# A sparse attention layer on one core: list extraction with three segments a quarter row, and later statistics, pinned scans and scatters

## The chip, the cores and the metric

The kernel runs on 1 core of one Trainium2 chip. The metric is device microseconds of one execution. Three runs of the kernel before gave 1813.75, 1815.98 and 1820.42 us; the median is 1815.98 us. One further execution was taken by the hardware profiler, and everything below that speaks of a place in time counts from the start of its span.

## The reference

One transformer layer over a graph of 4096 nodes, D = 512, 8 heads of 64, all in float32. Keys and values come from `x`, queries from `h_target`; the edge mask is the integer matrix `adj` (4096 x 4096, about 17 ones in a row).

```python
hs = layer_norm(x);  ht = layer_norm(h_target)
q = ht @ Wq / 8;  k = hs @ Wk;  v = hs @ Wv          # (4096, 8, 64)
logits = where(adj != 0, q . k, -1e30)
ctx = softmax(logits) @ v
ht = layer_norm(ht + ctx @ Wo)
y = ht + gelu(ht @ W1) @ W2                          # 512 -> 2048 -> 512
out = normalise(x + y)
```

## The kernel before, in words

Only the edges that exist are computed. The first stage makes two things from HBM: `kvd`, a table with k and v of every source row (4 KB a row), and for every target row a list of its edges. The second stage takes target rows in tiles of 128, sorted by degree, fetches one k|v row per target and list place with an indirect DMA ("a gather", 128 rows of 4 KB, 512 KB), and does attention and the feed-forward part.

**k|v** (`project`, `source`, L861 to L961). A source tile of 128 rows is normalised, transposed, and multiplied with Wk and Wv on PE (L930); ACT copies the two products out of PSUM (L932), and a DMA that ACT issues stores them to `kvd` (L936). There are 32 such tiles. PSUM has three buffers for the products (`pq`).

**Lists** (`edges`, L717 to L762). A target tile's row of `adj` comes in four quarters of 1024 columns, 512 KB each, loaded by SP (L714). For each quarter ACT writes sign bytes and their row sum (L729), DVE views two bytes as one 16 bit word and multiplies it with the word's place in its segment (`lio`, L734), and a MAX8 takes the eight largest words of each segment (L736). With `SQ = 5` a quarter's 512 words make 5 segments of at most 103 words; the place of a word goes up in steps of two, so that one byte holds it. After four quarters, a tile's 4 x 5 x 8 words are parted into bytes (L743, L744), turned into column numbers `gid`, 320 wide (L748, L751), and three MAX8 with two MATCH_REPLACE8 between them give the 24 largest (L755, L757). What is left over is written to HBM (`rest_d`, L767), for the few rows with a longer list.

The 32 target tiles are two parts of 16 (A, B). After part A's lists comes `sort(0)` (L809 to L858): a counting sort by degree on DVE, with four small products on PE, then 16 scatters by POOL that write each row's record (degree, row number, the two layer norm factors, the list) to its sorted place (L854). Records are then loaded, sorted, by POOL (L980). Part B goes the same way in `sort(1)`, but its lists are made beside the attention of part A.

**Statistics of h_target** (`moments`, L796 to L803): DVE's mean and variance of each target row, for the layer norm factors of the record. Two tiles are done per list (L738), so that all 32 are ready with part A's 16 lists. The rows lie in four slots of a ring of 20 buffers of 512 KB; the same ring later holds the gathered rows.

**Attention** (`attention`, L1160 to L1253). Per three gathers (a "segment"): a DVE product with q (L1220), a DVE reduction to logits `lg` (L1225), ACT's exponential (L1229, or L1238 for a tile's first segment), weighting of v on DVE (L1184) and, for one row in three, on ACT (L1201, L1204), and sums on PE by transposing products into `cps` (L1192). A tile's last segment starts `finish` (output projection, second norm), which ends with `h2T` of a group of one or two tiles. The feed-forward part (`feed`: L1325, gelu L1328, L1334) runs on those groups, woven between the attention's instructions.

**What sets the order.** Streams of work are Python generators, each of which yields an estimated cost; `_weave` takes the stream that is least far on. The first weave (L1438) has `projections`, `prepare` (part A's lists, sort, records, the first two queries) and `fill` (the next `FILL = 5` lists of part B). The second (L1449) has attention, feed-forward, `other_lists` (the remaining 11 lists and `sort(1)`; it begins at `WAIT = 40`, its costs are multiplied by 1.5) and the last weights. The framework's scheduler may then move an instruction ahead on its engine, unless `tc.issue_after` ties it behind another one. Each engine runs its instructions in the order that comes out, and so does each issuing queue. The number of quarters that may be loaded ahead is set by `RINGED`: tiles below it use the 8 ring slots 0 to 7, later ones two other buffers (`wide`).

## Time and profile before

| what | us |
|---|---|
| median of three runs | 1815.98 |
| the profiled execution, its own time | 1817.49 |
| its span | 1815.5 |
| PE busy in the span | 1677.8 (92%) |
| DVE busy | 1436.5 (79%) |
| ACT busy | 1224.1 (67%) |
| POOL busy | 982.2 (54%) |
| last k\|v product on PE ends | 280.6 |
| last k\|v store issued by ACT | 290.6 |
| first gather issued by POOL | 296.6 |
| first feed-forward product on PE | 373.5 |
| part B's scatters | 627 to 665 |
| last gathers land, attention ends | about 1670 |

The page gives each engine's busy time, a row of 40 slices in which a digit is a slice's busy share in tenths, the groups of instructions with the mean time of one, and the idle time before a group with what ended most of it. A table by windows gives busy time per engine for stretches that one chooses. A timeline gives single instructions: start, duration, engine, line, operation, tiles, and in brackets how long the engine had been idle and who released it. PE's busy time has to be read with care, since ends of matmuls are modelled and they overlap; idle time of PE is safe to read.

### The profile page before, as it was taken

What the parts mean: (1) busy time and instruction counts of PE and PEld (TensorE: products, weight loads), DVE (VectorE), ACT (ScalarE), POOL (GpSimd) and SP (SyncE); (2) the same over time, 40 slices, a digit from 0 to 9 for tenths busy, and PEclk for the clock granted to TensorE, in tenths of its full rate; (3) what the DMA queues carried; (4) which work ended last, traced back from release to release, by engine and by line L of the source; (5) the groups of instructions that cost most, each with busy time, mean ns of one, the idle gap of its engine ahead of it and who ended that gap; (6) DMA issues with size and microseconds to landing.
All of it is one profiled execution on the core that took longest, in us unless ns stands there. A gap on an engine that the chain in (4) does not pass through costs nothing. (4 is left out here: it accounts for less than half of the span.)

```text
span 1815.5 us, 22973 instructions
## 1 busy us (share of the span) xinstructions
PE 1677.8 (92%) x7030; PEld 1097.9 (60%) x7030; DVE 1436.5 (79%) x2660; ACT 1224.1 (67%) x3121; POOL 982.2 (54%) x834
## 2 busy tenths in 40 slices
PE   7989984597999979999999989999999999999997
PEld 3434442465766656766776757666666666666664
DVE  6989876899999837777978989978878797988200
ACT  5767654487987736766778868877777676787311
POOL 1000144656566676766678788867575665763101
PEclk9999996698999989999999999999999999999998
DMA  9999968989887557777878878787776776774000
GB/s 344 366 380 372 344 198 319 404 287 332 271 305 256 201 173 243 258 255 267 273 263 302 293 260 295 249 285 250 241 266 222 248 251 238 244 248 153 18 6 26
DMA packets 140269, 463.26 MB, mean 255 GB/s; under 512 B 16500, under 2 KB 21672, under 8 KB 140136
## 3 DMA queue, kind: packets, MB, share of 16 engines
q0 software_dynamic: 96656, 342.64, 55.8%
q1 hardware_dynamic: 35664, 95.98, 15.0%
q10 hardware_dynamic: 7816, 23.08, 3.3%
q8 instruction: 58, 0.95, 0.2%
q14 instruction: 75, 0.61, 0.1%
HBM read 430.75 MB, written 30.89 MB: 254 GB/s over the span
## 5 line engine op out<-in xcount | busy, mean ns | idle before, releaser
L967 POOL DMA_INDIRECT kv<-kvd,rec x603 | 758.1, 1257 | 347.5 <-PE cps L1192 139.7
L1334 PE MATMUL po<-w,gt 128*128 128x512 f32 x1024 | 466.4, 598 | 16.2 <-ACT gt L1328 16.2
L1325 PE MATMUL pf<-h2T,w 128*128 128x256 f32 (+1 forms) x2176 | 465.9, 368 | 0.1
L1325 PEld LDWEIGHTS pf<-h2T,w 128*128 128x128 f32 x2176 | 389.3, 191 | 64.5 <-issue 20.3
L1220 DVE TENSOR_TENSOR kv<-kv,tq 128x1536 f32<-128x1536 f32 (+2 forms) x211 | 351.6, 1675 | 68.3 <-DMA kv<-kvd,rec 56.2
L1204 ACT ACTIVATE kv<-kv,pa 128x64 f32<-128x64 f32 x1520 | 391.0, 336 | 4.3
L1225 DVE TENSOR_REDUCE lg<-kv 128x24 f32<-128x1536 f32 (+2 forms) x211 | 350.1, 1666 | 1.4
L1334 PEld LDWEIGHTS po<-w,gt 128*128 128x128 f32 x1024 | 188.8, 192 | 212.4 <-issue 194.3
L1192 PEld LDWEIGHTS cps<-ident,kv 128*128 128x128 f32 x2008 | 240.2, 145 | 109.4 <-issue 59.2
L1192 PE MATMUL cps<-ident,kv 128*128 128x128 f32 x2008 | 264.5, 280 | 44.1 <-DVE kv L1184 24.5
L1184 DVE TENSOR_TENSOR kv<-kv,p 128x1024 f32<-128x1024 f32 (+1 forms) x211 | 251.0, 1193 | 22.8 <-ACT p L1229 20.3
L687 POOL TENSOR_TENSOR n_rs<-n_ve,mhalf 128x2 f32<-128x2 f32 (+2 forms) x51 | 50.8, 997 | 329.1 <-DVE n_ve L680 165.3
L729 ACT ACTIVATE kv<-kv 128x1024 uint8<-128x1024 int32 x128 | 134.9, 1056 | 100.0 <-DMA kv<-in_adj_dram 51.7
L1328 ACT ACTIVATE gt<-pf 128x512 f32<-128x512 f32 x128 | 76.4, 597 | 93.8 <-PE pf L1325 75.8
L1328 ACT ACT_TABLE_LOAD x104 | 133.4, 1283 | 1.7
L736 DVE MAX8 cand<-kv 128x8 uint16<-128x103 uint16 (+1 forms) x640 | 131.8, 252 | 0.8 <-DVE R L755 0.2
L930 PE MATMUL pq<-wk,h2T 128*128 128x512 f32 x256 | 120.8, 616 | 12.1 <-ACT tq L932 7.2
L1012 PE MATMUL t<-wq,tq 128*128 128x512 f32 x256 | 118.2, 605 | 5.6 <-ACT tq L1006 5.6
L930 PE MATMUL pq<-wv,h2T 128*128 128x512 f32 x256 | 115.5, 594 | 6.4 <-ACT kv L729 3.0
L1229 ACT ACTIVATE p<-lg 128x24 f32<-128x24 f32 (+2 forms) x179 | 39.2, 219 | 113.0 <-DVE lg L1225 88.8
L1116 PE MATMUL t<-wo,rb 128*128 128x512 f32 x256 | 115.2, 592 | 0.0
L930 PEld LDWEIGHTS pq<-wk,h2T 128*128 128x128 f32 x256 | 48.9, 197 | 69.9 <-issue 55.2
(160 smaller groups left out, 1582.2 us busy)
## 6 DMA issues: line engine op xcount, KB each, us to landing
kv<-in_adj_dram SPq DMA_DIRECT2D x128, 512.0 KB
kvd<-tq ACTq DMA_DIRECT2D x24, 512.0 KB
kv<-kvd,rec POOLq DMA_INDIRECT x603
kv<-in_L_gnn_h_target_dram SPq DMA_DIRECT2D x32, 256.0 KB
kv<-in_x_dram SPq DMA_DIRECT2D x15, 512.0 KB
rest_d<-gid SPq DMA_DIRECT2D x32, 160.0 KB
w<-in_L_gnn_W_dram SPq DMA_DIRECT2D x4, 1024.0 KB
kvd<-kv ACTq DMA_DIRECT2D x8, 512.0 KB
```

What stands on the lines that cost most here:

```text
L729: nc.scalar.activation(sg, a, AF.Sign, accum_out=dpart[:, i, h:h + 1])
L736: nc.vector.max(cand[:, h * SQ + s, :], wd[:, w0:w1])
L930: nc.tensor.matmul(pkv, hT[:, kc, j * P:(j + 1) * P], w[:, kc, :], start=kc == 0, stop=kc == KC - 1)
L967: nc.gpsimd.indirect_dma_start(out=dst, out_offset=None, in_=table[:, :], in_offset=bass.IndirectOffsetOnAxis(ap=idx, axis=0))
L1184: nc.vector.tensor_tensor(v4, v4, p[:, j0:j0 + m, :].unsqueeze(3) .to_broadcast([P, m, H, HD]), ALU.mult)
L1192: nc.tensor.matmul(cps[:, c, :], kv[:, j, D + c * P:D + (c + 1) * P], ident, is_transpose=True, start=j0 + j == 0 and c == 0, stop=j0 + n ...
L1204: newest[:] = [nc.scalar.mul(v, v, pa[:, hd:hd + 1]).ins]
L1220: nc.vector.tensor_tensor(kv[:, :n, :D], kv[:, :n, :D], tq[:, :D].unsqueeze(1).to_broadcast([P, n, D]), ALU.mult)
L1225: nc.vector.tensor_reduce(lg[:, :n, :], kv[:, :n, :D].rearrange("p j (h d) -> p j h d", h=H), AX.X, ALU.add)
L1325: nc.tensor.matmul(pf[:, k, :], w1[(f0 + k) // KC][:, kc, (f0 + k) % KC * P:((f0 + k) % KC + 1) * P], h2T[:, kc, :w], start=kc == 0, stop= ...
L1328: nc.scalar.activation(gt, pf, AF.Gelu_apprx_tanh)
L1334: nc.tensor.matmul(po[j], gt[:, k, j * P:(j + 1) * P], w2[(f0 + k) // KC][:, (f0 + k) % KC, :], start=False, stop=f0 + k == FC - 1, skip_g ...
```

## The change

It has six parts.

1. `SQ` goes from 5 to 3: segments of at most 171 words, so 3 instead of 5 MAX8 a quarter, and 192 instead of 320 candidates a tile. A word's place now goes up by one and is doubled when `gid` is made (an add becomes one instruction with a multiply and an add); the column offsets begin at -1.
2. Part A's 16 statistics of h_target are taken one per list. Part B's 16 are taken one per quarter in the first four lists of part B, from one ring slot with two halves; the layer norm factors of a part (`factors`) are made and copied to the records when that part's statistics are there.
3. A sign scan of part B's lists is tied behind the newest k|v store (or, in the second stage, behind ACT's newest weighting of v), and its multiplication on DVE behind the newest reduction to logits. `edges` yields twice per quarter.
4. `FILL` goes from 5 to 7, with the last two of them after the last k|v tile; `RINGED` goes from 20 to 21. The second stage begins its 9 remaining lists at `WAIT = 60`, with costs times 1.8.
5. The scatters of `sort(1)` are each tied behind the newest gather.
6. Part B's records are loaded by SP, not by POOL.

```diff
-    SQ = 5
+    SQ = 3
...
-                nc.gpsimd.iota(io[:, :SQ * WS], pattern=[[0, SQ], [2, WS]], base=1,
+                nc.gpsimd.iota(io[:, :SQ * WS], pattern=[[0, SQ], [1, WS]], base=1,
...
-            FILL = 5
-            RINGED = NA + FILL - 1
+            FILL = 7
+            RINGED = NA + FILL - 2
...
+            def behind(ins):
+                return tc.issue_after(ins[-1]) if ins else nullcontext()
...
-                    nc.scalar.activation(sg, a, AF.Sign, accum_out=dpart[:, i, h:h + 1])
+                    with behind(newest if i >= NA else []):
+                        nc.scalar.activation(sg, a, AF.Sign, accum_out=dpart[:, i, h:h + 1])
...
+                    yield 0.0 if i < NA else 1.0
                     wd = sg.bitcast(U16)
-                    nc.vector.tensor_tensor(wd, wd, lio, ALU.mult)
+                    with behind(logits):
+                        nc.vector.tensor_tensor(wd, wd, lio, ALU.mult)
...
-                    if h % 2 and moms:
+                    if moms and (h == 1 or i >= NA):
                         moments(moms.pop(0))
-                    yield 2.0
+                    yield 2.0 if i < NA else 1.0
...
-                nc.vector.tensor_add(gid, gid, dec)
+                nc.vector.scalar_tensor_tensor(gid, dec, 2.0, gid, op0=ALU.mult, op1=ALU.add)
...
             def hrow(i):
-                return ring[:, DEEP + i // 2 % 4, i % 2 * D:(i % 2 + 1) * D]
+                slot = DEEP + i // 2 % 4 if i < NA else DEEP + 3
+                return ring[:, slot, i % 2 * D:(i % 2 + 1) * D]
...
-                while asked and len(asked) > NT - 4 - i:
+                while asked and asked[0] <= (min(i + 3, NA - 1) if i < NA else i + 1):
                     ask(asked.pop(0))
...
                 for i in range(n):
-                    ins = nc.gpsimd.indirect_dma_start(
+                    with behind(issues):
+                        ins = nc.gpsimd.indirect_dma_start(
...
-                nc.gpsimd.dma_start(rec[:, :RW], recs_d[part][r0:r0 + P, :])
+                (nc.sync if part else nc.gpsimd).dma_start(rec[:, :RW], recs_d[part][r0:r0 + P, :])
...
-            WAIT = 40.0
+            WAIT = 60.0
...
+            def factors(part):
+                i0, n = PARTS[part]
+                rs, nm = rstd_of(wp, mvh[:, i0:i0 + n, :], n, "n0")
+                Rf = Rs[part].bitcast(F32)
+                nc.vector.tensor_copy(Rf[:, :, RST], rs)
+                nc.vector.tensor_copy(Rf[:, :, RST + 1], nm)
+
             def prepare():
                 yield from _take(ed, NA * steps)
                 ready.append("lists")
-                while moms:
-                    moments(moms.pop(0))
...
+                factors(0)
...
             def fill():
                 while not ready:
                     yield None
-                yield 9.0
-                for cost in _take(ed, FILL * steps):
-                    yield cost
+                yield 4.0
+                yield from _take(ed, (FILL - 2) * steps)
+                factors(1)
+                while not latest:
+                    yield None
+                yield from _take(ed, 2 * steps)
...
                 for cost in ed:
-                    yield 1.5 * cost
+                    yield 1.8 * cost
```

In the built program the order on the engines moves as follows. On ACT, before, 29 scans of part B stand ahead of the last k|v store and 4 more between it and the attention's first exponential, 33 quarters in all, more than the 20 of `fill`, because the scheduler drew scans of `other_lists` forward. After, 16 stand ahead of the last store and 12 between the first queries and the first exponential, 28 in all. In the attention, the scan of the last quarter stands about at segment 39 before and at segment 44 after. On DVE, part B's 16 statistics stand in one block between the first and the second half of `sort(0)`, and the power that makes their factors stands on POOL ahead of part A's 16 scatters. On SP, 12 of the 16 loads of part B's h rows stand in a row, each waiting for the statistics of the tile two before, with five quarters of `adj` behind them. On POOL, part B's scatters stand one or two between one to three gathers (before: 9, then 6, then 1 in a row). The order of PE's instructions is the same but for details.

## What the change should do to the time

> **What bounds the kernel now.** I read busy time first. TensorE (PE) is busy 1677.8 us of a 1815.5 us span, and the built program keeps PE's order and amount of work. So the time is PE's work plus PE's gaps, 137.7 us, and a part of the change is worth the PE gap that it closes. The chain of waits reaches back only through the last 3 us and says nothing here; I used the table by windows. Its columns: window, length, then busy time (and instructions) of PE, PE weight loads, DVE, ACT, POOL, then PE's granted clock, DMA share, GB/s.
>
> ```profile
> 20.00:260.00 240.00, 228.68 (x615) 106.12 (x613) 217.81 (x944) 168.12 (x312) 29.32 (x30) 0.99 0.95 344
> 260.00:300.00 40.00, 21.89 (x47) 9.76 (x48) 23.77 (x103) 20.57 (x41) 13.84 (x17) 0.79 0.76 239
> 300.00:340.00 40.00, 12.76 (x46) 8.81 (x45) 27.73 (x41) 11.62 (x39) 27.48 (x24) 0.63 1.02 400
> 340.00:460.00 120.00, 100.96 (x530) 75.21 (x531) 118.38 (x222) 90.84 (x260) 74.45 (x62) 0.88 0.89 321
> 460.00:660.00 200.00, 197.30 (x891) 136.01 (x890) 173.70 (x337) 154.21 (x383) 125.46 (x106) 1.00 0.71 242
> 660.00:680.00 20.00, 10.05 (x44) 6.54 (x43) 7.33 (x5) 5.98 (x14) 15.00 (x14) 0.74 0.73 248
> ```
>
> Subtract PE from the length: 11.3 us idle in 20 to 260; 18.1 and 27.2 at the handover from k|v to attention; 19.0 in the ramp to 460, where DVE is full (118.4 of 120); 2.7 in the next 200; 9.95 in one hole at 660. Of the rest, 25 us lie spread over 680 to 1680 and 24 at the two ends; no part of the change touches those. So it works on at most 88 us.
>
> Then I read ACT's timeline at the handover: start, duration, engine, line, operation, tiles, and in brackets the idle time before it and its releaser.
>
> ```profile
> 282.72 1.06 ACT L729 ACTIVATE kv<-kv 128x1024 uint8<-128x1024 int32 x1 [1.85 <-DVE cand L736]
> ...
> 288.93 1.06 ACT L729 ACTIVATE kv<-kv 128x1024 uint8<-128x1024 int32 x1 [2.57 <-DMA kv<-in_adj_dram]
> ...
> 289.99 0.57 ACT L932 COPY kv<-pq 128x512 f32<-128x512 f32 x1
> 290.58 0.33 ACTq L936 DMA_DIRECT2D kvd<-kv  x1
> ```
>
> The last k|v product ends at 280.6, but ACT, in order, stands in sign scans that wait for `adj` quarters, and stores at 290.6, 10 us late. POOL's first gather follows at 296.6, the first exponential at 312.1. Third, DVE and PE at the hole:
>
> ```profile
> 664.35 1.76 DVE L1220 TENSOR_TENSOR kv<-kv,tq 128x1536 f32<-128x1536 f32 x1 [9.37 <-DMA kv<-kvd,rec]
> ```
> ```profile
> 671.55 5.51 PE L1334 MATMUL po<-w,gt 128*128 128x512 f32 x8 [9.95 <-ACT gt L1328]
> ```
>
> POOL issues 9, 6 and 1 scatters in a row (L854, 1.3 us from start to start, 627 to 665); the gathers behind them are late, DVE waits, ACT's exponential waits for DVE, and the gelu behind it on ACT keeps PE idle.
>
> **What the Trainium skill says.** "Perfetto Trace Analysis", section "Optimization Strategy": a kernel with several regimes is judged by the gaps of the engine to be kept full, within each regime. That is the method above; the table agrees, PE being full at 460 and idle by half at 300. "VectorE: DVE Perf Modes", section on the TRN2 errata: an operation from SBUF pays a fixed cost per instruction. The trace agrees: MAX8 takes 252 ns at 103 elements and 478 at 320, that is 1.04 ns an element and about 145 ns fixed. "TensorE: Matmul & The Clock Gate", section "HAM oscillation": idle gaps lower PE's clock. Here it is 0.63 and 0.74 in the two windows with long gaps; so a closed gap may return slightly more than its length, which I don't count. "DMA: Bandwidth & Descriptors", section "Issuing engines are not separate DMA queues": another issuing engine saves only issue time. This trace alone can't test that.
>
> **1. Three segments.** The prices:
>
> ```profile
> L736 DVE MAX8 cand<-kv 128x8 uint16<-128x103 uint16 (+1 forms) x640 | 131.8, 252 | 0.8 <-DVE R L755 0.2
> L755 DVE MAX8 R<-gid 128x8 int32<-128x320 f32 x96 | 45.9, 478 | 0.0
> ```
>
> These overlap, so I cost by distance of starts: 0.17 us at 103 (five take 0.85), 0.39 at 320, hence 0.24 at 171 and 0.26 at 192. A quarter goes from 0.85 to 3 x 0.24 = 0.72; the seven 320-wide instructions of a list save 7 x 0.13 = 0.9; a list costs 1.44 us less DVE (7.9 to 6.5), and 32 lists 46 us. In 20 to 260 this hides: PE needs 32 tiles x 8.04 us plus 19 at the start and end = 276, whatever DVE does. It counts only in the ramp. If DVE's lists were not hidden in the first stage (DVE 91% there), up to 5 us more would come. The rest writes shrink from 160 to 96 KB each, 2 MB in all.
>
> **2. Later statistics.** 16 x 0.7 = 11 us DVE and 4.2 MB of loads leave part A's lists and go into the stretch from about 190, where the one slot lets two 256 KB loads pass per cycle. One lands in 2.4 us unloaded, 3 to 4 loaded, so 7 cycles of 4 to 5 us take 28 to 35 us and end at 218 to 230. Queued behind these loads on SP are five `adj` quarters; on DVE, the second half of `sort(0)`; on POOL, the scatters behind the factors' power. Sort's second half begins at 235.7 before, because its PE product stands behind 26 k|v tiles, so the chain is covered by 5 to 17 us. Price 0; from -3 (lists A end sooner, the 11.3 us shrink) to +6 (each cycle 1.5 us slower than I think).
>
> **3 and 4. Pinned scans, seven lists, later start.** Before, 29 scans of part B stand ahead of the last store and 4 between it and the first exponential. After, 16 and 12. From the 17th on, before, quarters come through two `wide` buffers, 10 of them in 34.4 us, 3.4 us each; the 16 now ahead of the store have ring slots and arrive in time. So ACT copies out the last product as it ends, 280 to 282, and gathers start 8 to 10 us sooner, at about 287. Against that stand 12 scans in front of the first exponential: 4 from the ring, 8 through `wide`, four pairs. Such a pair took 6.9 us beside k|v work; with gathers running, SP's six issues
>
> ```profile
> 297.01 31.88 SPq L714 DMA_DIRECT2D kv<-in_adj_dram  x6
> ```
>
> took 31.9 us, 10.6 a pair. Four pairs from about 285 thus land at 313 to 327. I take the first exponential at 320, against 312.1. Behind it on ACT wait the weighting of v and the gelu; on DVE the weighting L1184, which frees gathers; on PE `cps`. From the first exponential to the first feed-forward product it took 61.4 us before, of which DVE waited 6.2 for gathers and 5 went to lists; 50 remain for attention. Now 20 ring slots can be full of gathers (40 us of DVE work at 1.95 each) when the exponential comes, so the waits go; the 5 of lists fall into DVE's wait before the exponential; some three quarters more come into this stretch (+3), and a second segment's product and reduction can be done ahead of it (-3). So 320 + 50 + 3 - 3 = 370, against 373.5: -3. Bounds: -18 (the scans land before the gathers, exponential at 305) and +23 (rival two).
>
> **Ramp, 373 to 660.** By finer windows PE is idle 2.3 us in 400 to 430, 7.6 in 430 to 460, both with DVE at 100%, and 2.7 in 460 to 660: 12.6. DVE's attention work is 5.9 us a segment (three gathers), PE needs 7.7. Lists add 29 quarters x 1.98 us over segments 15 to 40 before, 2.3 a segment, sum 8.2, more than PE's; after, 36 x 1.6 us over segments 10 to 44, 1.6 a segment, sum 7.5, less than PE's. I take -6; bounds 0 and -12. ACT, 91 of 120 busy, gains waits (a pinned scan can stop the gelu behind it), so half is left.
>
> **5. Scatters pinned.** The work stays, 16 x 1.27 us, but one or two now stand between gathers; a gather is late by 2.5 us at most instead of 12. POOL is 63% busy there, so it catches up. I take -8 of 9.95; bounds -10 and 0 (the waits for DMA landings remain).
>
> **6. Records by SP.** Of 32 record loads with 593 ns issue each, 16 leave POOL, 9.5 us of a POOL with 37% slack. On SP a load stands behind `adj` loads only until segment 44. A wait of SP for a record's scatter could delay the loads behind it, but by then those are few. I take -1; from -3 to +1.
>
> **The sum.** -3 - 6 - 8 - 1 = -18. Against the profiled 1817.5 (2 us more than its span) that is 1799.5. The profiled execution lies 1.5 us above the median 1815.98, so I say 1798.
>
> **Rivals.** *One: the handover eats most of it.* The first exponential comes at 325 to 330, the feed-forward product at 376 to 382, +3 to +8, while ramp and hole give 3 + 6: 1810 to 1815 (all rivals counted from 1817.5 less 1.5). For: eight wide quarters stand where four were, and DMA is full there (share 1.02). Against: gathers start sooner and find an empty ring. Chance 0.22. *Two, slower: the scans ahead of the first exponential.* If all four pairs come at the loaded cadence or above and begin only behind the first gathers, they take 42 to 48 us from 290 and the exponential falls at 335 to 340: +26 at the handover, less 12 for ramp and hole, about 1830. It decides from a first exponential at 335 on, if the distance to the first feed-forward product stays. Against: gathers fill their slots, then must wait for attention, so the queue empties for `adj`. Chance 0.14. *Three: more is gained*, -18, -11 and -10: 1777. For: 48 us of gaps lie between 280.6 and 373.5. Chance 0.16. *That the change doesn't do what it says*: 33 quarters already stand ahead of the first exponential, so "seven lists ahead" is really fewer, 28; my step uses the counts, not the name.
>
> **The numbers.** The forecast's own range is 1790 to 1806, chance 0.48. About 0.5% is what a measurement can tell from no change, so faster means under 1806.9, slower over 1825.1. Faster: 0.48 + 0.16 = 0.64. Slower: 0.14, and 0.02 of rival one gone further, 0.16. Same: the other 0.20. The range holds the forecast, rival one and two thirds of rival three: 1774 to 1822.
>
> **What would show it.** Right: last store L936 at 279 to 283; first gather before 290; first L1238 at 314 to 325; first L1325 at 366 to 373; PE gaps under 8 us in the 190 us before the scatters; no PE gap over 3 us around part B's scatters; MAX8 of L736 near 323 ns, x384. Wrong: a first exponential past 325 (rival one) or 335 (rival two); sort's second half later than 240 (the statistics chain); PE gaps before 260 above 15 us; new PE gaps behind a gelu L1328 with a scan L729 in front of it.

## The result, and the profile after

The changed kernel takes 1832.33 us (median of 4 runs, 1830.94 to 1833.89), beside 1817.6 for the kernel before on the same chip. The ratio is 1.0075, with a 95% interval of 1.0059 to 1.0091. So it is slower by some 0.75%, 14 to 15 us, where 18 us less were forecast, and outside the range (1774 to 1822).

The page of the changed kernel first: its span and the busy time of each engine, then the row of PE in 40 slices.

```profile
span 1830.9 us, 22786 instructions
...
PE 1679.5 (92%) x7030; PEld 1099.0 (60%) x7030; DVE 1403.2 (77%) x2406; ACT 1220.5 (67%) x3119; POOL 968.6 (53%) x819
...
PE   7989993596999997999998989999999999999995
```

PE's work is the same within 2 us, DVE's is 33 us less, and the span is 15.4 us longer. The time went into PE's gaps, as the method of the prediction would have it. The same windows as before, with one added (columns as there: length, PE, PE weight loads, DVE, ACT, POOL, clock, DMA share, GB/s):

```profile
20.00:260.00 240.00, 226.10 (x607) 105.61 (x607) 181.28 (x698) 154.89 (x290) 28.39 (x29) 0.98 0.91 328
260.00:300.00 40.00, 25.50 (x60) 10.74 (x58) 25.93 (x102) 23.67 (x46) 24.05 (x29) 0.90 0.78 266
300.00:340.00 40.00, 9.85 (x44) 8.62 (x44) 31.98 (x67) 12.98 (x41) 15.14 (x14) 0.50 0.95 351
340.00:460.00 120.00, 91.10 (x476) 66.70 (x475) 110.96 (x202) 88.22 (x256) 77.50 (x60) 0.86 0.87 318
460.00:660.00 200.00, 198.41 (x894) 136.66 (x893) 174.05 (x316) 158.90 (x399) 112.37 (x96) 1.00 0.76 257
660.00:680.00 20.00, 20.00 (x99) 14.62 (x98) 12.66 (x13) 11.22 (x28) 8.80 (x9) 1.00 0.51 173
680.00:800.00 120.00, 108.14 (x483) 74.51 (x482) 84.64 (x98) 72.02 (x200) 90.06 (x77) 0.97 0.76 248
```

Three things are to be seen. In 20 to 260 DVE has 36.5 us less to do (181.3, was 217.8), and PE gets nothing from it: 13.9 us idle, was 11.3. The ramp from 340 to 460, where part of the gain was to be, has 28.9 us of gaps instead of 19.0, with DVE at 92% and not full. And the hole at 660 is gone, but 680 to 800 now has 11.9, where the kernel before had 1.7:

```profile
680.00:800.00 120.00, 118.33 (x544) 82.00 (x543) 90.73 (x112) 80.29 (x217) 81.86 (x68) 1.00 0.75 251
```

A part of the loss isn't in any of these windows. The last thing that POOL does in both kernels is the issue of the last output; the first fence is the kernel before, the second the changed one:

```profile
1806.68 1.04 POOL L1302 DMA_INDIRECT out_dram<-xt,tags  x1 [1.38 <-DVE flag L1372]
```
```profile
1813.18 1.04 POOL L1311 DMA_INDIRECT out_dram<-xt,tags  x1 [1.38 <-DVE flag L1381]
```

The work ends 6.5 us later, but the span ends 15.4 us later: from this line to the end it is 8.8 us before and 17.7 us after. In the trace's records of the sequencers (which the page doesn't count as busy), POOL spends that time in two steps at the end of the program, one that raises its DMA semaphores and a drain: 0.66 and 1.95 us before, 2.45 and 9.30 after.

Milestones of progress, read from the two traces by the same instruction on PE, say where the other 6.5 us are:

| | before | changed | later by |
|---|---|---|---|
| last k\|v product ends | 280.6 | 280.3 | -0.3 |
| last store issued | 290.6 | 280.9 | -9.7 |
| first gather issued | 296.6 | 284.5 | -12.1 |
| first exponential | 312.1 | 319.9 | +7.8 |
| first feed-forward product | 373.5 | 375.6 | +2.1 |
| 137th feed-forward product (L1325, now L1334) | 448.7 | 458.8 | +10.1 |
| 409th | 635.5 | 640.4 | +4.9 |
| 545th | 751.6 | 762.2 | +10.6 |
| last product | 1802.6 | 1809.1 | +6.5 |
| end of span | 1815.5 | 1830.9 | +15.4 |

### The profile page after: what moved, and what is told of

Read it like the earlier page. It is cut to its first block, busy times and chain, and to the rows that moved or that the text cites. A ratio compares the mean times of both kernels' runs of the same rounds, so it can differ in the third digit from the quotient of the medians.

```text
span 1830.9 us, 22786 instructions
## 1 busy us (share of the span) xinstructions
PE 1679.5 (92%) x7030; PEld 1099.0 (60%) x7030; DVE 1403.2 (77%) x2406; ACT 1220.5 (67%) x3119; POOL 968.6 (53%) x819
## 5 line engine op out<-in xcount | busy, mean ns | idle before, releaser
L1334 PE MATMUL pf<-h2T,w 128*128 128x256 f32 (+1 forms) x2176 | 467.2, 369 | 0.4 <-ACT h2T L1156 0.4
L1334 PEld LDWEIGHTS pf<-h2T,w 128*128 128x128 f32 x2176 | 390.2, 191 | 65.1 <-issue 20.1
L687 POOL TENSOR_TENSOR n_rs<-n_ve,mhalf 128x2 f32<-128x2 f32 (+2 forms) x52 | 46.0, 884 | 366.8 <-DVE n_ve L680 196.8
L742 DVE MAX8 cand<-kv 128x8 uint16<-128x171 uint16 (+1 forms) x384 | 108.8, 324 | 5.1 <-issue 3.0
L938 PEld LDWEIGHTS pq<-wv,h2T 128*128 128x128 f32 x256 | 49.6, 195 | 71.9 <-issue 59.4
```

Source lines behind the costliest of these rows:

```text
L938: nc.tensor.matmul(pkv, hT[:, kc, j * P:(j + 1) * P], w[:, kc, :], start=kc == 0, stop=kc == KC - 1)
L1334: nc.tensor.matmul(pf[:, k, :], w1[(f0 + k) // KC][:, kc, (f0 + k) % KC * P:((f0 + k) % KC + 1) * P], h2T[:, kc, :w], start=kc == 0, stop= ...
```

## The experiments

Seventeen kernels ran. Names with a are edits of the changed kernel, with b of the kernel before. Each ratio is against the kernel before, measured beside it on the same chip. To compare with the changed kernel, compare with its ratio, 1.0075; it was not measured again beside the edits, so such a difference is one of two ratios with an interval each, and under some 0.2% it says nothing. The columns in between are from one profiled execution each.

| run | edit | k\|v ends | first exp | first feed-forward | PE idle 373 to 540 | POOL's two end steps | median us | ratio (interval) |
|---|---|---|---|---|---|---|---|---|
| before | | 280.6 | 312.1 | 373.5 | 11.4 | 2.6 | | 1 |
| changed | | 280.3 | 319.9 | 375.6 | 17.6 | 11.8 | 1832.3 | 1.0075 (1.0059 to 1.0091) |
| a1 | records by POOL | 280.1 | 320.6 | 376.8 | 16.9 | 2.6 | 1824.8 | 1.0049 (1.0033 to 1.0065) |
| b1 | part 6 alone | 275.8 | 309.0 | 370.5 | 11.6 | 11.8 | 1820.9 | 1.0032 (1.0019 to 1.0045) |
| a2 | part 4 undone | 277.4 | 298.9 | 369.6 | 17.4 | 11.8 | 1836.5 | 1.0133 (1.0114 to 1.0152) |
| a3 | part 5 undone | 278.2 | 317.9 | 373.7 | 17.0 | 11.8 | 1841.2 | 1.0142 (1.0125 to 1.0159) |
| b2 | part 1 alone | 274.0 | 301.8 | 364.9 | 21.5 | 2.6 | 1820.8 | 1.0040 (1.0025 to 1.0054) |
| a4 | part 3 undone | 294.1 | 325.7 | 388.9 | 19.8 | 11.8 | 1858.9 | 1.0254 (1.0229 to 1.0280) |
| b3 | part 5 alone | 276.5 | 309.7 | 370.4 | 11.0 | 2.6 | 1817.6 | 1.0026 (1.0010 to 1.0043) |
| a5 | last record by POOL | 277.9 | 320.3 | 376.5 | 17.0 | 1.1 | 1826.0, one run | |
| a6 | part 2 undone | 266.0 | 306.6 | 362.4 | 16.9 | 11.8 | 1820.6 | 1.0039 (1.0024 to 1.0053) |
| a7 | ten record buffers | 274.6 | 318.9 | 375.4 | 17.2 | 11.8 | 1831.0 | 1.0102 (1.0077 to 1.0128) |
| a8 | 24 scans ahead of the store | 281.9 | 308.4 | 368.6 | 13.2 | 11.8 | 1822.5 | 1.0062 (1.0045 to 1.0079) |
| a9 | a8, a7 and a1 | 281.2 | 308.4 | 368.2 | 9.6 | 2.6 | 1808.4 | 0.9969 (0.9957 to 0.9981) |
| a10 | parts 2 and 6 undone | 266.4 | 306.9 | 362.8 | 15.9 | 2.6 | 1815.3 | 1.0000 (0.9986 to 1.0014) |
| a11 | a9 with part 2 undone | 274.5 | 296.5 | 354.2 | 12.7 | 2.6 | 1796.0 | 0.9883 (0.9856 to 0.9910) |
| b4 | part 2 alone | 288.8 | 318.8 | 384.5 | 18.1 | 2.6 | 1837.1 | 1.0110 (1.0084 to 1.0136) |
| a12 | part 2 with four slots | 283.1 | 324.2 | 379.9 | 19.2 | 11.8 | 1837.0 | 1.0112 (1.0087 to 1.0137) |
| a13 | part B's h rows not loaded | 269.6 | 309.9 | 366.1 | 16.4 | 11.8 | 1830.3 | 1.0089 (1.0074 to 1.0104) |

How far one profile can be trusted: kernels whose k|v stage is the same (before, b1 and b3; changed, a1, a3, a5 and a7) end it at 275.8 to 280.6 and at 274.6 to 280.3. So a difference of up to 6 us in one milestone alone proves nothing.

**The end of the program (a1, b1, a5).** a1 takes part 6 out of the changed kernel, b1 puts it alone into the kernel before:

```diff
-                (nc.sync if part else nc.gpsimd).dma_start(rec[:, :RW], recs_d[part][r0:r0 + P, :])
+                nc.gpsimd.dma_start(rec[:, :RW], recs_d[part][r0:r0 + P, :])
```

> The changed kernel with part B's records loaded by POOL again (part 6 undone). In the changed kernel's last 18 us POOL spends 2.45 us in the step that raises its DMA semaphores and 9.30 us in a drain, against 0.66 and 1.95 before: 9.1 us of the 15.4 lost. Theory: the 16 loads taken from POOL's own queue change what that drain has to wait for. Then the two fall to about 0.7 and 2.0 and the time to 1823 (1821 to 1825). Rival: the tail belongs to another part (pinned scatters, smaller rest rows); then they stay at 2.4 and 9.3 and the time stays at 1832, give or take 2 for the records' own waits.

> The kernel before with part B's records loaded by SP (part 6 alone). Theory of the queue: the end grows by 9 us, time 1826 (1824 to 1828). Rival, the tail belongs to another part: drain stays at 2.0, time 1816 to 1819.

The two end steps are 0.66 and 1.95 in a1, 2.45 and 9.30 in b1. They are 11.8 us in every kernel of the table that has the whole of part 6, and 2.6 in every one without it. The time followed as well, by ratio with less than 9 us: a1 is 0.26% (4.7 us) below the changed kernel, b1 0.32% (5.8 us) above the kernel before. What do the steps depend on? a5 loads the very last record by POOL again:

```diff
-                (nc.sync if part else nc.gpsimd).dma_start(...)
+                (nc.sync if part and i < NT - 1 else nc.gpsimd).dma_start(...)
```

> The changed kernel with the very last record of part B loaded by POOL, the other 15 by SP. What does the long end depend on? If on how recently POOL issued a plain load, the drain is back at about 2 us and the time at 1823; if on the number of such loads that POOL issued in all (17 instead of 16), drain and raise stay at 9.3 and 2.4 and the time at 1832.

They fell to 0.36 and 0.73 us, below even the kernel before. So the count alone (17 plain loads by POOL here, 16 in the changed kernel) doesn't make the long end. What goes with it in all these kernels is how late the last plain load comes: 115 indirect DMAs of POOL follow it in a5 and before, 200 in a9 and a11, 512 to 615 in the kernels with the long end. What the two steps do in that time no trace shows, and why 32 plain loads give a drain of 1.95 and 17 give 0.73 is open.

**The handover (a2).** Part 4 undone, so that only 20 scans stand ahead of the first exponential, none of them through the `wide` buffers:

```diff
-            FILL = 7
-            RINGED = NA + FILL - 2
+            FILL = 5
+            RINGED = NA + FILL - 1
...
-                yield from _take(ed, (FILL - 2) * steps)
+                yield from _take(ed, FILL * steps)
                 factors(1)
-                while not latest:
-                    yield None
-                yield from _take(ed, 2 * steps)
...
-            WAIT = 60.0
+            WAIT = 40.0
...
-                    yield 1.8 * cost
+                    yield 1.5 * cost
```

> The changed kernel with part 4 undone (five lists ahead, ring limit 20, second stage at 40 with factor 1.5); pins and three segments stay. By the built order 20 scans of part B stand ahead of the first exponential, none of them from the two wide buffers. Theory: the eight scans from the wide buffers cost the handover; without them the first exponential comes at 298 to 304 instead of 319.9 and the first feed-forward product at 352 to 360 instead of 375.6, while eight more quarters in the attention cost DVE 8 x 1.6 = 13 us and give part of it back: total 1816 to 1826. Rival: the handover is limited by the gathers' bytes, not by the scans; then the first feed-forward product stays within 4 us of 375.6 and the time is 1832 or more.

The exponential came at 298.9, as expected, 21 us earlier. The first feed-forward product came only 6 us earlier, which was expected of neither theory, and the time rose by 0.6%, as the rival said. The windows of a2 show why:

```profile
300.00:340.00 40.00, 19.07 (x83) 16.04 (x84) 33.04 (x47) 17.99 (x65) 24.72 (x20) 0.55 1.03 404
340.00:360.00 20.00, 8.94 (x43) 5.16 (x41) 19.12 (x47) 13.03 (x39) 11.32 (x11) 0.83 1.03 408
```

DMA is full (share 1.03) and DVE nearly so, since the eight quarters now fall here: from the trace, 10.2 us of DVE's time in 340 to 373.5 is list work, none in the kernel before. Scans that are taken out ahead of the exponential are paid for behind it. Whether they cost less ahead of the last store is what a8 asks.

**Scans ahead of the store (a8).** In a8 all seven lists come ahead of the end of k|v in the weave, at half their cost. The pins stay, and 28 quarters still stand ahead of the first exponential, 24 of them ahead of the last store:

```diff
-                yield from _take(ed, (FILL - 2) * steps)
-                factors(1)
-                while not latest:
-                    yield None
-                yield from _take(ed, 2 * steps)
+                for cost in _take(ed, FILL * steps):
+                    yield 0.5 * cost
+                factors(1)
```

> The changed kernel with the costs of the seven lists halved and all seven ahead of the end of k|v in the order: 24 scans (not 16) ahead of the last store, 4 (not 12) between it and the first exponential, 28 in all as before; pins as they are. Theory: the price of the change is the 12 scans that stand between store and exponential while ACT and DVE have slack earlier (DVE idle 66 us in 20 to 280). Then the last store stays at 280 to 285, the first exponential falls from 320 to 300 to 308, and the time to 1820 to 1825, 9 of it the longer end. Rival: DMA is the limit (share 1.0 from 300 to 360), so an earlier exponential only waits for gathers: first feed-forward product within 4 us of 375.6, time 1829 or more.

The exponential came at 308.4 and the time at 1822.5, near what the first theory said; but the store slipped to 287.5, and by the ratio (1.0062) the difference to the changed kernel lies within the two intervals. Alone, it proves little; in a11 it counts.

**The pins (a4).**

```diff
-                    with behind(newest if i >= NA else []):
+                    if True:
                         nc.scalar.activation(sg, a, AF.Sign, accum_out=dpart[:, i, h:h + 1])
...
-                    with behind(logits):
+                    if True:
                         nc.vector.tensor_tensor(wd, wd, lio, ALU.mult)
```

> The changed kernel with part 3 undone (scans and multiplications not tied to stores or reductions). The built order then has 35 scans of part B ahead of the last store and 40 ahead of the first exponential, against 16 and 28. Theory: what the pins cost is that DVE stood idle 66 us in 20 to 280 (30 before), and 13 quarters were moved into a stretch where DVE and DMA are full. Without pins the last store is late, 292 to 300, but the ramp has little list work: first feed-forward product at 368 to 378, PE gaps in 373 to 660 under 6 us instead of 18, time 1814 to 1822, with the 9 us of the longer end still in it. Rival: twelve scans through two buffers are simply too many ahead of the first exponential, pinned or not; then the first exponential comes at 325 or later and the time is 1832 or more.

1858.9: my theory that the pins cost fell, by 40 us. With 35 scans free to move ahead of the last store, ACT waits in scans that stand in front of evictions, and k|v itself ends at 294.1. Two waits of PE in that stretch of a4; the scan ahead of the first had waited 6.7 us for its quarter of `adj`, the one ahead of the second 5.0 us for DVE:

```profile
259.74 5.80 PE L938 MATMUL pq<-wv,h2T 128*128 128x512 f32 x8 [5.29 <-ACT kv L940]
276.47 5.40 PE L938 MATMUL pq<-wk,h2T 128*128 128x512 f32 x8 [3.19 <-ACT h2T L923]
```

So the pins are worth 1.8% to a kernel that has seven lists ahead.

**Three segments alone (b2).** The edit is part 1 of the diff, put into the kernel before.

> The kernel before with part 1 alone (three segments). The built order keeps 29 scans ahead of the last store and 33 ahead of the first exponential. Theory: the ramp is bound by DVE (list work 21 us in 400 to 460), so 27 percent less list work takes PE's gaps of 9.9 us there to 5 or less: 1809 to 1813. Rival: ACT and the adj loads set it, not DVE: 1815 to 1818, no change.

Neither theory was right: it is slower by 0.4%. Its first feed-forward product comes 8.6 us earlier, but then four scans follow each other closely on ACT, three of which wait 3.4 to 5.0 us for their quarters, with a gelu and an exponential behind them, and PE has 10.5 us of gaps in 460 to 540 (1.4 before). Two of the three, on ACT:

```profile
506.77 1.06 ACT L729 ACTIVATE kv<-kv 128x1024 uint8<-128x1024 int32 x1 [3.42 <-DMA kv<-in_adj_dram]
...
511.71 1.06 ACT L729 ACTIVATE kv<-kv 128x1024 uint8<-128x1024 int32 x1 [3.79 <-DMA kv<-in_adj_dram]
```

So cheaper lists let unpinned scans bunch here. In the changed kernel, which pins them, PE has 0.7 us of gaps in 460 to 540; parts 1 and 3 without the others didn't run.

**The scatters (b3, a3).** b3 puts part 5 alone into the kernel before, a3 takes it out of the changed one (the `with behind(issues):` of the diff).

> The kernel before with part 5 alone (part B's scatters each tied to the newest gather). The prediction's step: the PE hole of 9.95 us at 660 shrinks to 2 or less, time 1806 to 1809. Rival, seen in the changed kernel: POOL stands at the first scatter until its ranks are there, and PE loses as much in several smaller gaps: 1814 to 1818.

> The changed kernel with part 5 undone (scatters of part B not tied to a gather). Theory: pinning put the first scatter in POOL's order ahead of its ranks, so that POOL stood 9.1 us and gathers behind it were late; PE lost 9.0 us in 700 to 800. Unpinned, one hole of about 10 us returns near the scatters, so the balance is near zero: 1831 to 1834. Rival, pinning saves what the prediction said: 8 us worse, 1840.

b3 bears out the rival, and by the ratio is even a little slower. PE at 660 to 760 in b3:

```profile
660.00:700.00 40.00, 38.08 (x160) 24.90 (x159) 19.14 (x23) 16.71 (x46) 31.08 (x28) 0.96 0.74 241
700.00:760.00 60.00, 51.85 (x232) 36.25 (x231) 47.18 (x55) 41.43 (x113) 39.02 (x33) 0.94 0.65 214
```

The hole of 9.9 us is 1.9, and the next 60 us have 8.1 instead of 1.7: 8.0 saved, 6.4 given back. In the changed kernel it is the same (11.8 us of gaps in 660 to 820, 14.9 before). a3 however is 0.67% slower than the changed kernel, which the theory "near zero" didn't expect; its gaps in 660 to 820 are 9.9, so the loss isn't there. It lies at 1000 to 1400 (18.4 us of gaps, 12.5 in the changed kernel), 300 us after the last scatter. In that stretch DVE waits 21.9 us for layer norm powers, which POOL runs behind queued gathers (16.8 in the changed kernel, the longest single wait 10.3 and 6.6); but a10 has such a wait of 10.3 too and isn't slow, so the cause stays open.

**The later statistics (a6, b4, a12, a13).** a6 takes part 2 out of the changed kernel, b4 puts it alone into the kernel before.

> The changed kernel with part 2 undone (all statistics with part A's lists, as before). In the changed kernel the twelve h loads in a row keep SP from 208.8 to 230.9, and part B's first scan runs at 232 instead of 203. Theory: that chain delays the lists, so without it more scans are done early, the handover is shorter, and the time is 1822 or less. Rival: the order on ACT is tied by the pins (16 scans ahead of the last store in this kernel too), so the chain only fills a wait: 1830 to 1836.

> The kernel before with part 2 alone. Theory: the later statistics themselves cost stage one, whatever the segments and pins: last k|v product later than in the kernel before by 5 or more, time 1820 to 1828. Rival: they cost only together with the pinned scans, which can't run ahead while the chain of loads holds SP; then 1811 to 1817.

The first theory held in both: 0.36% less in a6, and in b4 k|v ends 8 us later; b4's time, 1.1% more, is even 9 us above what was expected. In a6 k|v ends at 266.0, 14 us earlier than in the changed kernel, with the same 16 scans pinned ahead of the store. In b4 there is one large wait that shows its mechanism. POOL, then DVE, then ACT, then PE of b4:

```profile
245.77 1.17 POOL L855 DMA_INDIRECT rec<-R,kv  x1 [51.04 <-DVE kv L852]
...
264.93 0.96 POOL L855 DMA_INDIRECT rec<-R,kv  x1 [0.30 <-issue]
265.92 2.94 POOL L687 TENSOR_TENSOR n_rs<-n_ve,mhalf 128x16 f32<-128x16 f32 x1
```
```profile
268.89 0.18 DVE L692 SCALAR_TENSOR_TENSOR n_nm<-mvh,n_rs 128x16 f32<-128x16 f32 x1 [14.85 <-POOL n_rs L687]
```
```profile
270.60 1.06 ACT L729 ACTIVATE kv<-kv 128x1024 uint8<-128x1024 int32 x1 [10.82 <-DVE cand L736]
```
```profile
272.74 5.75 PE L931 MATMUL pq<-wk,h2T 128*128 128x512 f32 x8 [9.21 <-ACT h2T L916]
```

The power for part B's factors sits on POOL behind the 16 scatters, DVE stands 14.9 us for it, ACT's scan 10.8 for DVE, PE 9.2 for an eviction behind that scan. In the changed kernel the power stands ahead of the scatters, so this wait isn't there. What is there is DVE waiting for h rows. The waits of DVE in 20 to 282, changed kernel, then a6:

```profile
DVE n_st L697 <- DMA kv<-in_L_gnn_h_target_dram: 22.9, 15, 4.2
DVE n_st L697 <- DMA kv<-in_x_dram: 13.3, 5, 4.1
```
```profile
DVE n_st L697 <- DMA kv<-in_x_dram: 6.3, 5, 2.8
DVE n_st L697 <- DMA kv<-in_L_gnn_h_target_dram: 4.4, 4, 1.8
```

Two runs tried this cause. a12 gives part B's rows the four slots that part A had, loads them seven ahead, and keeps the k|v products in their own tiles until then. a13 leaves the loads out.

```diff
-                slot = DEEP + i // 2 % 4 if i < NA else DEEP + 3
-                return ring[:, slot, i % 2 * D:(i % 2 + 1) * D]
+                return ring[:, DEEP + i // 2 % 4, i % 2 * D:(i % 2 + 1) * D]
...
-                while asked and asked[0] <= (min(i + 3, NA - 1) if i < NA else i + 1):
+                while asked and asked[0] <= (min(i + 3, NA - 1) if i < NA else i + 7):
...
-                    if moms and moms[0] < NA:
+                    if moms:
```

> The changed kernel with part B's statistics as late as there, but their rows in four ring slots, loaded up to seven ahead, and the k|v products kept in their own tiles until all statistics are done. Theory, the chain through one slot costs (DVE waited 22.9 us for h rows in the changed kernel, 4.4 in run a6): most of the 12 us return, 1820 to 1824. Rival, the cost comes from moving 11 us of DVE work and the loads behind part A's lists at all: 1829 to 1834.

```diff
-                nc.sync.dma_start(hrow(i), h_target[i * P:(i + 1) * P, :])
+                if i < NA:
+                    nc.sync.dma_start(hrow(i), h_target[i * P:(i + 1) * P, :])
```

> The changed kernel without the 16 loads of part B's h rows (4.2 MB): part B's statistics are computed, at the same places in DVE's order, from the rows of part A that still lie in the slot, so part B's layer norm factors are not the reference's. It takes away what DVE and SP wait for (22.9 us of DVE before the h rows in the changed kernel) and leaves the work. Theory, the cost of part 2 is these waits: k|v ends at 266 to 270 as in run a6, time 1820 to 1823. Rival, it is the place of the work and what goes wrong ahead of it: k|v ends at 276 or later and the time is 1828 or more.

a12 gave nothing back. Its last row load is issued by 214.6 (230.9 in the changed kernel), and DVE waits 12.5 us for rows instead of 22.9; k|v ends at 283.1 all the same. So neither the single slot nor the length of the chain is the cause. a13 split its two predictions. Without the loads DVE's wait for rows is 5.4 us, and k|v ends at 269.6 and the first feed-forward product at 366.1, as the first theory said; but the time is the rival's, 1830.3. The lead of 9 to 11 us is still there at 751 and is then lost in 820 to 1400, where PE has 26.4 us of gaps (19.8 in the changed kernel, 20.5 in a6), in a stretch whose instructions the edit doesn't touch. But the edit did not leave the work at its places, though the expectation says so. With no loads to wait for, DVE makes part B's statistics at 171 to 198 (205 to 234 in the changed kernel), the first four ahead of part A's last multiplication, and on ACT an eviction at 187 stands ahead of a normalisation (L899 of the changed kernel) which it follows there. So a13 shows that k|v ends 5 to 11 us earlier (the five kernels with the changed k|v stage end it at 274.6 to 280.3) when loads and order change together, not that the loads alone do it.

PE's own gaps in k|v say where the time goes. The two longest in 150 to 282, changed kernel:

```profile
196.40 4.05 PE L938 MATMUL pq<-wv,h2T 128*128 128x512 f32 x5 [3.05 <-ACT tq L940]
...
268.02 5.37 PE L938 MATMUL pq<-wv,h2T 128*128 128x512 f32 x8 [3.21 <-ACT kv L940]
```

The first gap lies at 193.4 to 196.4, and SP issues the first of part B's row loads at 196.1, so they can't have caused it: the eviction stands on ACT behind that normalisation, which waited 7.7 us for the factors of its rows of x (in a6 and a13 it stands ahead). All ten kernels that have the changed kernel's part 2 with its loads have 2.2 to 3.4 us of gaps in 190 to 200; a6, a10 and a11, without part 2, have none, and a13 has 0.2. From 208 to 234, while SP stands in the chain of loads and DVE waits for rows, PE has no gap at all. Before the second gap ACT waited 5.4 us, and the trace names nothing on this core that ended it; a5 and a7, the same kernel up to there, don't have this gap. So the waits for rows cost PE nothing where they stand, and the order on ACT at 190 to 200 is one part of what part 2 costs. That this is the whole isn't shown.

**The record wait (a7).** `bufs=6` becomes `bufs=10` for the records.

> The changed kernel with ten buffers for records instead of six. At 420 to 430 POOL stands 9.0 us at a record load whose buffer is still in use, and the queries behind it come 5 us late for PE. Theory: this wait makes 5 of the 11 us of PE gaps in 430 to 460; without it the time is 1825 to 1828. Rival: DVE and the gathers are the limit there and the gaps stay: 1831 to 1833.

Nothing came of it alone, though it also lets some scatters move by a place (12.8 us of gaps in 430 to 460, 11.3 in the changed kernel).

**Together (a9, a10, a11).** a9 is a8 with records by POOL and ten record buffers. a10 undoes parts 2 and 6 of the changed kernel. a11 is a9 with part 2 undone.

> Kernel a8 with records by POOL and ten record buffers: if the three costs add (9 of the end, 8 of the handover, 5 of the record wait), 1810 to 1814, as good as or better than the kernel before; if they overlap, 1816 to 1822.

> The changed kernel with part 2 (later statistics) and part 6 (records by SP) both undone. If their costs add (12 from run a6, 7.5 from run a1, out of 1832), the time is 1811 to 1815, at or below the kernel before, and no other part need be blamed for the loss. If they overlap, 1817 to 1822.

> The changed kernel with parts 2 and 6 undone, ten record buffers, and 24 scans ahead of the last store instead of 16: run a9 with early statistics. If the 12 us of part 2 and the gain of a9 add, 1796 to 1801; if an earlier end of k|v only lets the scans ahead of it run later, 1805 to 1810.

All three came within 2 us of the range of the first case. a9 is 0.31% faster than the kernel before. a10 equals it (1.0000), so parts 2 and 6 together account for the measured loss: by ratio 0.36% and 0.26% singly, 0.75% together, which adds within the intervals. a11 is the fastest, 1796.0 us, 1.2% below the kernel before. The lists ahead of the last store, with the ten record buffers, are worth 0.8% in a9 beside a1 and 1.2% in a11 beside a10; the two were not parted there. The windows of a11:

```profile
260.00:300.00 40.00, 24.13 (x48) 10.38 (x48) 30.26 (x108) 21.33 (x48) 20.45 (x22) 0.76 0.87 311
300.00:340.00 40.00, 24.80 (x119) 18.60 (x120) 36.48 (x38) 18.84 (x71) 29.03 (x24) 0.69 1.03 404
340.00:460.00 120.00, 100.16 (x510) 71.69 (x509) 113.31 (x222) 95.05 (x257) 73.29 (x58) 0.91 0.85 307
```

At 300 to 340, where PE did 12.8 us of work before and 9.9 in the changed kernel, it does 24.8.

## Why the prediction was wrong, step by step

**The method held.** PE's work stayed, the loss is PE's gaps, and the rest is after PE's last product. Its first claim failed in one number, though: "PE needs 32 tiles x 8.04 us plus 19 = 276, whatever DVE does". In a6 the last fourteen tiles take 7.3 us each, and k|v ends at 266. The 8.04 came from tiles that had small gaps in them. So stage one was not at PE's limit, and what stands around PE's work there did count. A second claim failed too: that no part of the change touches the gaps in 680 to 1680 and at the two ends. 680 to 800 alone has 10 us more of them, and the end 9.

**Step 1, three segments: price right, cover wrong.** MAX8 of a segment was put at 323 ns:

```profile
L742 DVE MAX8 cand<-kv 128x8 uint16<-128x171 uint16 (+1 forms) x384 | 108.8, 324 | 5.1 <-issue 3.0 <-DVE kv L740 1.0
```

DVE's saving is there, 33 us by busy time (46 were worked out by the distance of starts), but the work around it decides where it goes: in b2 into bunched scans, in the changed kernel into idle time of DVE in 20 to 260.

**Step 2, later statistics: this step failed.** It was priced at 0, with -3 to +6, because the chain of loads (predicted to end at 218 to 230, measured 233) was covered against the second half of the sort. The cover was true of the sort, and the scatters began at 244.8, 1.6 us later than before. Measured: k|v ends 14 us earlier when part 2 is undone (a6, a10), 0.36% of the time, some 6.5 us (a6); and 1.1% is lost when it is put into the kernel before (b4), there with POOL's power behind the scatters. The prediction did name POOL's queue and judged only that the power stands ahead of the scatters. On SP everything behind the twelve loads stood too,

```profile
208.76 22.13 SPq L802 DMA_DIRECT2D kv<-in_L_gnn_h_target_dram  x12
```

and DVE stood in its own order in front of each row. The first scan of part B ran at 232.0, 223 in a6, 203 before (227 in a13, which has no such loads). But PE has no gap while this lasts, so the chain that the step worried about isn't what cost. The step's mistake is that it asked only how long the chain is, and took k|v as bound by PE whatever moves around it; the trace shows PE waiting for evictions in another order on ACT, at 196.

**Steps 3 and 4, handover: the mechanism right, the size off by 5.** Last store 280.9 (forecast 280 to 282), first gather 284.5 (287), first exponential 319.9 (320). From there to the first feed-forward product it took 55.7 us, not 50. By the trace 6.5 us of DVE in 320 to 373 are list work (3 were counted), and the head start of 3 didn't come: one product and one reduction were done ahead of the exponential, 3.4 us, no more than before. The gathers could not use their 12 us. POOL filled the ring and then stood until the first sums on PE freed a slot:

```profile
305.77 0.94 POOL L976 DMA_INDIRECT kv<-kvd,rec  x1 [0.30 <-issue]
327.27 1.58 POOL L976 DMA_INDIRECT kv<-kvd,rec  x1 [20.56 <-PE cps L1201]
```

The step saw the full ring and counted it as a gain ("the waits go"), not as 20 us in which no gather is issued; DMA's share in 300 to 340 is 0.95, and was 1.02 before.

**The ramp: failed, +6 where -6 was forecast.** PE's gaps in 373 to 660 are 18.4 us, 12.6 before; at the 137th feed-forward product the delay has grown by 8. DVE's average per segment was worked out as below PE's, and so it is: DVE has idle time in 373 to 460. But PE's gaps are now made by single waits, those of which the prediction said "a pinned scan can stop the gelu behind it" and then took half. PE in 410 to 460:

```profile
420.89 5.40 PE L1343 MATMUL po<-w,gt 128*128 128x512 f32 x8 [3.89 <-ACT gt L1337]
441.67 2.47 PE L1201 MATMUL cps<-ident,kv 128*128 128x128 f32 x12 [2.91 <-DVE kv L1193]
449.08 1.11 PE L1012 MATMUL t<-ident,tq 128*128 128x128 f32 x4 [4.95 <-ACT tq L1008]
452.60 0.69 PE L1152 MATMUL t<-ident,h 128*128 128x128 f32 x2 [2.41 <-ACT h L1143]
```

The first is that gelu, behind two scans of which one waited 1.8 us for its quarter. The third looked like the record load that held POOL for 9.0 us, but a7 took that wait's buffer limit away and the gaps stayed. The step's own lever, less list work for DVE, wasn't there. From the first to the 137th feed-forward product DVE does 11 segments in both kernels and, by distance of starts, 19.9 us of list work, 20.3 before: 1.8 us a segment in both, where 1.6 and 2.3 were taken. Nor does its amount alone decide: a8, a9 and a11 have 18.8 to 19.2 us of it and take 76 to 79 us for this stretch; all nine kernels with 12 scans between the last store and the first exponential take 82 to 86 (75 before), and a2, with 23.4 us of list work, 84. So the ramp answers to where those scans stand; by which wait isn't shown. Half of the delay is given back by 640; the last list's scan runs at 611.

**Step 5, scatters: the saving right, its return overlooked.** -8 was forecast for the hole, 8.0 was saved in b3, and 6.4 came back behind it. POOL's queue stays long for 70 us (scatters from 673 to 743, were 627 to 664), and a layer norm's power waits in it: DVE stood 7.8 us for it at 711, 3.0 before. A cost that is spread over a queue isn't gone when the queue has other users.

**Step 6, records by SP: failed, +9 where -1 was forecast.** The step looked for waits in the attention, and none came. It cited "DMA: Bandwidth & Descriptors" of the Trainium skill, section "Issuing engines are not separate DMA queues", that only issue time is saved; that is not contradicted. The cost is in the end of the program, which the prediction had set aside and its sum didn't hold at all: two steps of POOL that grew from 2.6 to 11.8 us, of which the time shows 0.26 to 0.32% (a1, b1).

**The rivals.** The slower rival had nearly the right time, 1830, and the wrong reason: it needed a first exponential at 335 or later. It came at 319.9. Rival one's mark, a first feed-forward product at 376 to 382, was nearly met (375.6); with its gains of 9 for ramp and hole it would have been 1810 to 1815.

**What stays open.** How part 2 makes up its whole cost: a12 rules out the slot and the length of the chain, PE's gaps rule out the waits for rows, the order on ACT at 190 to 200 is one part, and b4's power acts in b4 alone. Which wait makes the ramp slow. And what makes PE's gaps in 820 to 1400 differ by up to 9 us (17.5 in a8, 26.4 in a13) between kernels whose edits touch nothing there, which took a13's lead and made a3 slow.

## What to carry to other kernels

Before a stage is called bound by one engine, take that engine's cadence from a stretch without gaps; here it was 7.3 and not 8.04 us a tile. Work that is moved out of a stage must be priced where it lands, with the order that it leaves on every engine there and with each small step behind other work on a queue (b4's power); a wait of an engine that isn't the bottleneck, as DVE's for rows, can be long and cost nothing. And waits that a change spreads must be looked for after the place where they vanish. A bundle should be undone part by part: here two of six parts made the whole loss, one (pins) was worth 1.8%, and with those two out, the lists moved ahead of the last store and ten record buffers, the rest gave 1.2%.

## What the runs showed of the hardware that was not expected

The end of a program on POOL isn't constant: its two last steps took 11.8 us when its last plain (not indirect) load lay 512 or more indirect DMAs back (16 plain loads in all), 2.6 us with 115 or 200 and 32 plain loads, 1.1 us with 115 and 17 (a5). So it changed with which engine issued loads of 14.5 KB hundreds of us earlier. A power of 16 factors per row took POOL 2.9 us (changed kernel, b4), of 32 factors 5.4 (before, a6). And k|v's end moved by up to 6 us between kernels that do the same up to there, so a milestone needs more than one profile.
